# A transformer block in float32 on one core: large products split into four column tiles

## The chip, the cores and the metric

The kernel runs on one core of a Trainium2 chip. The metric is the device time of one execution in microseconds, the median over several runs. The core has a matrix engine (TensorE, "PE" in the profile, its weight loads "PEld"), a vector engine (DVE), a scalar engine (ACT), GpSimd (POOL) and a queue engine (SP) that starts most transfers.

## The reference

The kernel computes one pre-norm transformer block over 16 sequences of 256 tokens with 256 features, all in float32:

```python
def reference(x, wq, wk, wv, wo, gate_cp, up_cp, down_cp):
    x = x + attn(layernorm(x), wq, wk, wv, wo)
    return x + ffn(layernorm(x), gate_cp, up_cp, down_cp)

def attn(x, wq, wk, wv, wo):                 # 16 heads of 16
    q, k, v = x @ wq.T, x @ wk.T, x @ wv.T   # split in heads
    scores = einsum("bihd,bjhd->bhij", q, k) * 16 ** -0.5
    scores = where(j - i > 16, -inf, scores) # no key over 16 ahead
    return einsum("bhij,bjhd->bihd", softmax(scores), v) @ wo.T

def ffn(h, gate_cp, up_cp, down_cp):         # inner width 1024
    gate_w, up_w, down_w = (spline(cp) for cp in ...)  # cubic splines through control points
    return (silu(h @ gate_w.T) * (h @ up_w.T)) @ down_w.T
```

## The kernel before

One sequence is a batch b. The weights of the feed-forward part are made once at the start from the control points (`spline`) and stay in SBUF. The rest is a software pipeline: the loop over s (20 steps) does, in each step, stages of several batches that are at different points of their way. An order written out by hand says which stage stands where: within a step there are seven gaps between blocks of scores, and `project` and `fill` put the other products into them. Every engine runs its instructions in the order in which they are written (`InOrder`), so this order is what each engine does.

A full step has on PE, roughly: scores (`inner`), values (`values`, tile po), gate and up products (`gate_up`, tiles pg and pu), scores, query and key products (`project_part`, pq and pk), scores (`outer`), pg and pu, scores, po, pg and pu, scores, output projection (`project_o`, py), first half of the down product (`down`, pd), scores, second pd, transposes of the normed tokens (`turn_f`, ptf), value projection (`project_v`, pv), transposes of the maxima (`turn_max`, pm), pg and pu. For the first seven batches the normed input is transposed on PE too (`turn_a`, pta); later ones load a transposed input and are scaled afterwards. Three small sums of weights (`sum_weights`) occur once.

PE works on these in different shapes. The scores use 16 or 17 rows (the head's width, and one more for the maximum) and 64 columns, eight in the array side by side. The values use 128 rows and 32 columns, four side by side: the four heads of a group write to partitions 0, 32, 64 and 96 of the tile po:

```python
pe.matmul(
    po[32 * r : 32 * r + 32, gg, i : i + n],
    lhsT=vs[b % NQK][:, c, 4 * g + r, :],
    ...
```

All the large products use the whole array, 128 rows by 128 columns, with 256 columns streamed, and the transposes of normed tiles use `pe.transpose`, a matrix instruction in a transposing mode, against the tile `ident`. In the profile a float32 product shows as two instructions, a transpose as one.

PSUM is shared by pools: two tiles for the scores (`ps_s`), two buffers for pg, pu, pd and the splines (`ps_f`), two for everything else (`ps_m`). ACT computes the exponentials (e), the tanh of the gate (th) and several copies; DVE the row maxima (z), the gate's products (th, inter) and the residual sums.

Of the kernel before, what the change touches and what calls it, by code (L numbers as in the profile page):

```python
# [18 lines left out]
P = 128  # L19
# [74 lines left out]
def block_kernel(  # L94
# [14 lines left out]
    pe, dve, act, pool, sp = (  # L109
        InOrder(tc, e) for e in (nc.tensor, nc.vector, nc.scalar, nc.gpsimd, nc.sync)  # L110
    )
# [21 lines left out]
    xTs = {}  # L133
# [7 lines left out]
    w_in = {}  # L141
# [28 lines left out]
    ident = const.tile([P, P], F32, tag="ident", name="ident")  # L170
# [3 lines left out]
    means = const.tile([P, P], F32, tag="means", name="means")  # L174
# [37 lines left out]
    downT = const.tile([P, 8, DIM], F32, tag="downT", name="downT")  # L212


    xns, mxs, aus, aos, recs, x2s, x2Ts = ({} for _ in range(7))
# [15 lines left out]
    def normed(b, nm):  # L231
# [6 lines left out]
            )  # L238
        return xn

    def copied(engine, dst, src):
        (act.copy if engine is act else dve.tensor_copy)(dst, src)

    def transposed(src, dst, nm, engine=act):

        pt = ps_m.tile([P, 2, S], F32, tag="m", name=f"p{nm}")
        for kc in range(2):
            for c in range(2):
                pe.transpose(
                    pt[:, kc, c * P : (c + 1) * P],  # L250
                    src[:, c, kc * P : (kc + 1) * P],
                    ident,
                )
        copied(engine, dst, pt)


# [11 lines left out]
    def turn_a(b, engine=act):  # L268
        xTs[b] = sb3.tile([P, 2, S], F32, tag="xT", name=f"xT{b}")
        transposed(xns.pop(b), xTs[b], f"ta{b}", engine)  # L270

    sums = {}

    def sum_weights(nm):
        sums[nm] = ps_f.tile([P, DIM], F32, tag="f", name=f"sum{nm}")
        for kc in range(2):
            pe.matmul(
                sums[nm], lhsT=means, rhs=w_in[nm][:, kc, :], start=(kc == 0), stop=(kc == 1)
            )

    def center(nm):
        for kc in range(2):
# [16 lines left out]
    def project_part(b, i):  # L299

        if i == 0:
            qkcs[b] = sb.tile([P, 2, 2, S], F32, tag="qkc", name=f"qkc{b}")
        nm, qkc = "qk"[i], qkcs[b]
        pq = ps_m.tile([P, 2, S], F32, tag="m", name=f"p{nm}{b}")
        for oc in range(2):
            for kc in range(2):
                pe.matmul(
                    pq[:, oc, :],
                    lhsT=w_in[nm][:, kc, oc * P : (oc + 1) * P],
                    rhs=xTs[b][:, kc, :],  # L310
                    start=(kc == 0),
                    stop=(kc == 1),
                )
        if b < RAW:
            act.copy(qkc[:, i], pq)
        else:
            dve.tensor_tensor(
                qkc[:, i], pq, across[b].unsqueeze(1).to_broadcast([P, 2, S]), ALU.mult
            )

    def project_qk(b):
        project_part(b, 0)
        project_part(b, 1)
# [11 lines left out]
    def project_v(b, engine=act):  # L335
        pv = ps_m.tile([P, 2, DIM], F32, tag="m", name=f"pv{b}")
        for c in range(2):
            for kc in range(2):
                pe.matmul(
                    pv[:, c, :],  # L340
                    lhsT=xTs[b][:, kc, c * P : (c + 1) * P],
                    rhs=w_in["v"][:, kc, :],
                    start=(kc == 0),
                    stop=(kc == 1),
                )
        for c in range(2):
            to = vs[b % NQK][:, c, :, 0:HD]
            heads = pv[:, c, :].rearrange("p (h d) -> p h d", d=HD)
            if b < RAW:
                copied(engine, to, heads)  # L350
            else:
                act.activation(to, heads, AF.Copy, scale=factors[b][:, c : c + 1])
        del xTs[b]
# [177 lines left out]
    def project_o(b):  # L531
        py = ps_m.tile([P, 2, DIM], F32, tag="m", name=f"py{b}")
        ao = aos.pop(b)
        for c in range(2):
            for kc in range(2):
                pe.matmul(
                    py[:, c, :],
                    lhsT=ao[:, kc, c * P : (c + 1) * P],
                    rhs=w_in["o"][:, kc, :],
                    start=(kc == 0),  # L540
                    stop=(kc == 1),
                )
        dve.tensor_tensor(xs[b], xs[b], py, ALU.add)

# [6 lines left out]
    def turn_f(b):  # L551
        x2Ts[b] = sb.tile([P, 2, S], F32, tag="x2T", name=f"x2T{b}")
        transposed(x2s.pop(b), x2Ts[b], f"tf{b}")


    def gate_up(b, i):
        if i == 0:
            inters[b] = sb1.tile([P, 8, S], F32, tag="inter", name=f"inter{b}")
        pp = []
        for nm, w in (("g", gateT), ("u", upT)):  # L560
            t = ps_f.tile([P, 2, S], F32, tag="f", name=f"p{nm}{b}_{i}")
            for ic in range(2):
                for kc in range(2):
                    at = (2 * i + ic) * P
                    pe.matmul(
                        t[:, ic, :],
                        lhsT=w[:, kc, at : at + P],
                        rhs=x2Ts[b][:, kc, :],
                        start=(kc == 0),
                        stop=(kc == 1),  # L570
                    )
            pp.append(t)
        th = sb.tile([P, 2, S], F32, tag="th", name=f"th{b}_{i}")
        act.activation(th, pp[0], AF.Tanh, scale=0.5)
        dve.scalar_tensor_tensor(th, th, 1.0, pp[0], ALU.add, ALU.mult)
        dve.tensor_tensor(inters[b][:, 2 * i : 2 * i + 2, :], th, pp[1], ALU.mult)

    pds = {}

    def down(b, c, half=None):  # L580

        inter = inters[b]
        if half != 1:
            pds[b, c] = ps_f.tile([P, DIM], F32, tag="f", name=f"pd{b}_{c}")
        for ic in range(8) if half is None else range(4 * half, 4 * half + 4):
            pe.matmul(
                pds[b, c],
                lhsT=inter[:, ic, c * P : (c + 1) * P],
                rhs=downT[:, ic, :],
                start=(ic == 0),  # L590
                stop=(ic == 7),
            )
        if half == 0:
            return
        dve.tensor_tensor(xs[b][:, c, :], xs[b][:, c, :], pds.pop((b, c)), ALU.add)
        to = out[b].rearrange("(c p) d -> p c d", p=P)
        if b == B - 1:
            sp.dma_start(to[:, c, :], xs[b][:, c, :])
        elif c == 1:
            sp.dma_start(to, xs.pop(b))  # L600
# [48 lines left out]
    def fill(s, gap):  # L649


        if s < B - AHEAD:
            order = (
                (1, gate_up, 1), (3, gate_up, 2), (4, gate_up, 3), (5, down, 0), (6, down, 1),
            )
        else:
            order = (
                (1, gate_up, 1), (2, gate_up, 2), (3, gate_up, 3), (4, down, 0, 0),
                (5, down, 0, 1), (6, down, 1, 0), (6.5, down, 1, 1),
            )  # L660
        for at, stage, *what in order:
            if at == gap:
                do(stage, s - 4, *what)
        if gap == 7:
            do(gate_up, s - 3, 0)
# [3 lines left out]
    def part(i):  # L669
# [6 lines left out]
            (stats_a, 2), (scores_and_values, 2),  # L676
        ),
        (0, 4): ((turn_a, 1, dve), (project_v, 0, dve), (norm_a, 2), (part, 0)),
        (1, 1): ((turn_a, 2), (project_part, 1, 0), (stats_a, 3)),
        (1, 2): ((project_part, 1, 1), (spread, 1), (coefficients, 1)),  # L680
        (1, 3): ((project_qk, 2), (spread, 2), (norm_a, 3), (scores_and_values, 3)),
        (1, 4): ((project_v, 1), (stats_a, 4)),
        (1, 5): ((turn_a, 3), (part, 1), (norm_a, 4), (coefficients, 2)),
        (1, 6): ((project_qk, 3),),
        (1, 7): (
            (spread, 3), (stats_a, 5), (norm_a, 5), (project_v, 2), (part, 2),
            (scores_and_values, 4),
        ),
# [8 lines left out]
        (3, 2): ((project_qk, 6), (spread, 6)),  # L697
        (3, 3): ((project_v, 4), (project_v, 5)),
        (3, 6): ((project_v, 6), (sum_weights, "q"), (sum_weights, "k")),
        (3, 7): ((center, "q"), (center, "k")),  # L700
        (4, 1): ((sum_weights, "v"), (center, "v")),
    }

# [27 lines left out]
    for s in range(B + 4):  # L731
# [20 lines left out]
        fill(s, 4)  # L752
        inner(nb, tb, 3)
        do(project_o, ob)
        do(stats_f, ob)
        project(s, 5)
# [46 lines left out]
```

## Time and profile before

| | |
|---|---|
| time, median of 3 runs | 657.59 us (655.72 to 658.88) |
| the profiled execution, its own time | 656.36 us |
| its span, first to last instruction | 654.3 us |
| PE busy, matrix instructions | 644.9 us, 7380 |
| PEld busy | 501.3 us |
| DVE, ACT, POOL busy | 369.0, 216.3, 129.5 us |
| granted clock of TensorE | 1.000 |
| PE's program fetched (queue q8) | 58 packets, 0.95 MB |
| large products in the timeline: pg, pu, pd | 512 instructions each |
| pq, pk, pv, py | 128 instructions each |
| ptf and pta; pm | 64 and 28; 32 |
| po; scores | 1024; 4096 |

Nearly all instructions carry line 88, that of the helper `InOrder`, so groups are told apart by the names of their tiles: "pg<-x2T,gateT" writes pg from x2T and gateT. The form stands behind it: 128*32 is an instruction on 128 rows and 32 columns of the array, and 128x256 says what it streams. Matrix instructions overlap, so the lengths that the timeline gives run into each other; what a stage takes is read from its start to the start of the next one.

### The profile page before, as it was taken

How to read it: one execution, taken by the hardware profiler on the slowest of the kernel's cores; microseconds unless marked ns; L12 is line 12 of the kernel's file. 1: busy time of each engine (PE TensorE's matmuls, PEld its weight loads, DVE VectorE, ACT ScalarE, POOL GpSimd, SP SyncE). 2: the span in 40 equal slices, each digit the busy share in tenths (PEclk: the TensorE clock that was granted, in tenths of full speed). 3: DMA queues.
4: the chain of work that ended last, by engine and by line, in shares of the span. 5: the costliest groups of instructions: out<-in, count | busy, mean ns of one | idle time of the engine just before them, and what ended most of it. 6: DMA issues, size and time to landing. Idle time of an engine off the chain costs nothing.

```text
span 654.3 us, 18421 instructions
## 1 busy us (share of the span) xinstructions
PE 644.9 (99%) x7380; PEld 501.3 (77%) x7380; DVE 369.0 (56%) x1482; ACT 216.3 (33%) x383; POOL 129.5 (20%) x254
## 2 busy tenths in 40 slices
PE   8999999999999999999999999999999999999998
PEld 6666667877878777787877778787777777777886
DVE  6785566656464665646566464655656564733342
ACT  1345533233332323333232333323333333333110
POOL 6232222211111221112121121211212030212000
PEclk9999999999999999999999999999999999999999
DMA  5844132214132231413213131210010101010100
GB/s 170 174 69 63 46 64 65 46 37 87 31 75 42 45 65 36 86 33 73 44 36 75 36 71 33 56 31 18 21 34 20 33 23 31 23 36 19 50 17 16
DMA packets 40612, 33.18 MB, mean 51 GB/s; under 512 B 10576, under 2 KB 39888, under 8 KB 40528
## 3 DMA queue, kind: packets, MB, share of 16 engines
q1 hardware_dynamic: 39392, 30.97, 21.3%
q8 instruction: 58, 0.95, 0.6%
q10 hardware_dynamic: 1136, 1.05, 0.6%
q14 instruction: 26, 0.21, 0.3%
HBM read 14.42 MB, written 4.47 MB: 29 GB/s over the span
## 4 chain that ended last, share of the span: by engine, by line
PE 89%; DVE 1%; ACT 1%; issue 0%; POOL 0%; ACTq 0%
PE pg L88 18%; PE pd L88 17%; PE pu L88 17%; PE scores L88 14%; PE po L88 7%; PE py L88 5%; PE pv L88 3%; PE pq L88 3%; PE pk L88 3%; PE ptf L88 1%; PE pw L88 1%; PE pm L88 0%; ACT e L88 0%; DVE z L88 0%; DVE x L88 0%
## 5 line engine op out<-in xcount | busy, mean ns | idle before, releaser
L88 ACT ACTIVATE e<-scores 128x512 f32<-128x512 f32 (+1 forms) x192 | 117.5, 615 | 273.1 <-PE scores L88 224.5
L88 DVE CUSTOM_DVE_ANT_0 z<-scores,mask 128x144 bf16<-128x144 f32 (+1 forms) x512 | 154.7, 362 | 55.5 <-PE scores L88 32.7
L88 POOL TENSOR_SCALAR_AFFINE_SELECT e<-e 128x224 f32<-128x224 f32 (+1 forms) x192 | 93.8, 489 | 407.2 <-ACT e L88 404.4
L88 PE MATMUL pg<-x2T,gateT 128*128 128x256 f32 x512 | 125.5, 388 | 0.1
L88 PE MATMUL pu<-x2T,upT 128*128 128x256 f32 x512 | 121.0, 379 | 0.0
L88 PE MATMUL pd<-downT,inter 128*128 128x256 f32 x512 | 119.4, 383 | 0.0
L88 DVE SCALAR_TENSOR_TENSOR th<-th,pg 128x512 f32<-128x512 f32 x64 | 44.0, 687 | 117.5 <-ACT th L88 117.5
L88 PE MATMUL scores<-qk 17*64 17x144 f32 (+7 forms) x4096 | 106.2, 317 | 1.6 <-ACT e L88 1.1
L88 PEld LDWEIGHTS pg<-x2T,gateT 128*128 128x128 f32 x512 | 92.5, 190 | 19.7 <-DVE mx L88 4.7
L88 PEld LDWEIGHTS pu<-x2T,upT 128*128 128x128 f32 x512 | 97.3, 190 | 13.2
L88 PEld LDWEIGHTS pd<-downT,inter 128*128 128x128 f32 x512 | 95.2, 190 | 14.5 <-DVE mx L88 0.9
L88 PEld LDWEIGHTS scores<-qk 17*64 17x64 f32 (+1 forms) x4096 | 68.8, 131 | 37.3 <-issue 31.1
L88 ACT ACTIVATE th<-pg 128x512 f32<-128x512 f32 x64 | 38.2, 597 | 69.8 <-PE pg L88 69.2
L88 DVE TENSOR_TENSOR inter<-th,pu 128x512 f32<-128x512 f32 x64 | 44.0, 688 | 26.2 <-PE pu L88 26.2
L88 PE MATMUL po<-e,v 128*32 128x256 f32 (+1 forms) x1024 | 50.0, 336 | 0.0
L88 PEld LDWEIGHTS po<-e,v 128*32 128x32 f32 x1024 | 29.5, 109 | 23.3 <-issue 12.3
L88 DVE DVE_READ_ACCUMULATOR2_ANT mx<- 128x1 f32 x512 | 42.6, 83 | 0.1
L88 DVE TENSOR_TENSOR x<-x,pd 128x256 f32<-128x256 f32 x32 | 13.4, 420 | 41.2 <-PE pd L88 39.9
L88 PE MATMUL pq<-xT,wq 128*128 128x256 f32 x128 | 31.7, 390 | 0.7 <-ACT xT L88 0.7
L88 PE MATMUL py<-wo,ac 128*128 128x256 f32 x128 | 31.9, 392 | 0.0
L88 PE MATMUL pv<-wv,xT 128*128 128x256 f32 x128 | 30.7, 384 | 0.4 <-ACT qkc L88 0.4
L88 PE MATMUL pk<-xT,wk 128*128 128x256 f32 x128 | 30.6, 381 | 0.0
(69 smaller groups left out, 382.9 us busy)
## 6 DMA issues: line engine op xcount, KB each, us to landing
qk<-qkc SPq DMA_DIRECT2D x124, 64.0 KB
x<-x SPq DMA_DIRECT2D x16, 256.0 KB
ac<-au SPq DMA_DIRECT2D x128, 32.0 KB
rb<-rd SPq DMA_DIRECT2D x32, 128.0 KB
out<-x SPq DMA_DIRECT2D x15, 256.0 KB
xT<-xT SPq DMA_DIRECT2D x9, 256.0 KB
fa<-ra SPq DMA_DIRECT2D x9, 128.0 KB
qk<-mxT SPq DMA_DIRECT2D x64, 4.0 KB
```

What stands on the lines that cost most here:

```text
L88: return self.tc.keep_in_program_order(fn(*args, **kwargs))
```

## The change

A helper `product` writes one large product as four matrix instructions, for the columns 0 to 31, 32 to 63, 64 to 95 and 96 to 127 of its stationary operand; each writes its 32 partitions of the output. The moving operand is the same for all four. `project_part`, `project_v`, `project_o`, `gate_up`, `down` and `sum_weights` call it. The transposes of normed tiles (`transposed`, called by `turn_a` and `turn_f`) become products with `ident` as the moving operand, by the same helper. `turn_max` keeps its transposes, the splines and the few warm-up products at the start (`keep_running`) keep their forms, and the scores and values are as they were.

```diff
+    def product(out, lhsT, rhs, start, stop):
+        for at in range(0, P, 32):
+            pe.matmul(
+                out[at : at + 32], lhsT=lhsT[:, at : at + 32], rhs=rhs, start=start, stop=stop
+            )
+
+    def turned(out, src):
+        product(out, src, ident, True, True)
+
...
-                pe.transpose(
-                    pt[:, kc, c * P : (c + 1) * P],
-                    src[:, c, kc * P : (kc + 1) * P],
-                    ident,
-                )
+                turned(pt[:, kc, c * P : (c + 1) * P], src[:, c, kc * P : (kc + 1) * P])
...
-                    pe.matmul(
-                        t[:, ic, :],
-                        lhsT=w[:, kc, at : at + P],
-                        rhs=x2Ts[b][:, kc, :],
-                        start=(kc == 0),
-                        stop=(kc == 1),
+                    product(
+                        t[:, ic, :], w[:, kc, at : at + P], x2Ts[b][:, kc, :], kc == 0, kc == 1
                     )
...
-            pe.matmul(
-                pds[b, c],
-                lhsT=inter[:, ic, c * P : (c + 1) * P],
-                rhs=downT[:, ic, :],
-                start=(ic == 0),
-                stop=(ic == 7),
+            product(
+                pds[b, c], inter[:, ic, c * P : (c + 1) * P], downT[:, ic, :], ic == 0, ic == 7
             )
```

The other calls (pq, pk, pv, py and the sums) are changed in the same way.

More of the change, by code (lines that the diff above doesn't have):

```diff
@@ L276, in sum_weights @@
         for kc in range(2):
-            pe.matmul(
-                sums[nm], lhsT=means, rhs=w_in[nm][:, kc, :], start=(kc == 0), stop=(kc == 1)
-            )
+            product(sums[nm], means, w_in[nm][:, kc, :], kc == 0, kc == 1)
     def center(nm):
@@ L306, in project_part @@
             for kc in range(2):
-                pe.matmul(
-                    pq[:, oc, :],
-                    lhsT=w_in[nm][:, kc, oc * P : (oc + 1) * P],
-                    rhs=xTs[b][:, kc, :],
-                    start=(kc == 0),
-                    stop=(kc == 1),
+                product(
+                    pq[:, oc, :], w_in[nm][:, kc, oc * P : (oc + 1) * P], xTs[b][:, kc, :],
+                    kc == 0, kc == 1,
                 )
@@ L338, in project_v @@
             for kc in range(2):
[L339 to L344, printed above, removed]
+                product(
+                    pv[:, c, :], xTs[b][:, kc, c * P : (c + 1) * P], w_in["v"][:, kc, :],
+                    kc == 0, kc == 1,
                 )
@@ L535, in project_o @@
             for kc in range(2):
[L536 to L541, printed above, removed]
+                product(
+                    py[:, c, :], ao[:, kc, c * P : (c + 1) * P], w_in["o"][:, kc, :],
+                    kc == 0, kc == 1,
                 )
@@ L564, in gate_up @@
                     at = (2 * i + ic) * P
-                    pe.matmul(
-                        t[:, ic, :],
-                        lhsT=w[:, kc, at : at + P],
-                        rhs=x2Ts[b][:, kc, :],
-                        start=(kc == 0),
-                        stop=(kc == 1),
+                    product(
+                        t[:, ic, :], w[:, kc, at : at + P], x2Ts[b][:, kc, :], kc == 0, kc == 1
                     )
@@ L585, in down @@
         for ic in range(8) if half is None else range(4 * half, 4 * half + 4):
-            pe.matmul(
-                pds[b, c],
-                lhsT=inter[:, ic, c * P : (c + 1) * P],
-                rhs=downT[:, ic, :],
-                start=(ic == 0),
-                stop=(ic == 7),
+            product(
+                pds[b, c], inter[:, ic, c * P : (c + 1) * P], downT[:, ic, :], ic == 0, ic == 7
             )
```

## The prediction

> **What bounds the kernel now.** I read the page from the top: the share of each engine, then the chain that ended last, then the groups of the matrix engine, and last its timeline over one full batch.
>
> ```profile
> span 654.3 us, 18421 instructions
> PE 644.9 (99%) x7380; PEld 501.3 (77%) x7380; DVE 369.0 (56%) x1482; ACT 216.3 (33%) x383; POOL 129.5 (20%) x254
> PEclk9999999999999999999999999999999999999999
> ...
> PE 89%; DVE 1%; ACT 1%; issue 0%; POOL 0%; ACTq 0%
> ```
>
> PE is busy in 99% of the span at its full granted clock (1.000 in the view of the cores), and nearly all of the chain is PE. No other engine comes near: whatever PE's stages gain or lose goes into the end time one for one, if the other engines keep their slack. So the question is what PE does between useful columns. The timeline of PE shows it (start, length, instructions; the lengths overlap, so I read start to start):
>
> ```profile
> 304.17 1.89 PE L88 MATMUL pu<-x2T,upT 128*128 128x256 f32 x8
> 305.99 1.04 PE L88 MATMUL scores<-qk 16*64 16x208 f32 x32
> 306.96 1.56 PE L88 MATMUL po<-e,v 128*32 128x256 f32 x32
> 308.45 1.99 PE L88 MATMUL pg<-x2T,gateT 128*128 128x256 f32 x8
> 310.28 1.89 PE L88 MATMUL pu<-x2T,upT 128*128 128x256 f32 x8
> ...
> 319.52 3.72 PE L88 MATMUL pd<-downT,inter 128*128 128x256 f32 x16
> 323.08 0.60 PE L88 MATMUL ptf<-ident,xnf 128*128 128x128 f32 x4
> 323.51 1.89 PE L88 MATMUL pv<-wv,xT 128*128 128x256 f32 x8
> 325.24 0.38 PE L88 MATMUL pm<-ident,mx 128*16 128x128 f32 x2
> 325.46 1.89 PE L88 MATMUL pg<-x2T,gateT 128*128 128x256 f32 x8
> ```
>
> Three forms of the array alternate: 128*128 (the large products and transposes), 128*32 (po, the values: four side by side), 16*64 and 17*64 (scores). Each logical f32 product is two instructions (8 in a stage of four products). pv between ptf and pm takes 323.51 to 325.24, 1.73 us for 8: 216 ns each, no gap. pg after po takes 308.45 to 310.28, 1.83: about 0.10 more. pu before the scores takes 304.17 to 305.99, 1.82: about 0.09 more. These tenths are changes of form.
>
> The single starts in the trace make them exact; they repeat to within a few ns all along the span.
> - From the last start of a 128*128 stage to the scores: 309 ns, so 93 beyond its 216. All 94 such exits lie between 93 and 106.
> - From the scores' last columns to a large product: 86 (68 times). Then the product's first instruction takes 320 ns instead of 216: 104 of exposed weight load (128 columns). A transpose exposes 56 (3 times).
> - From the scores to po: 86 (31 times), and then only 24 of exposed load (32 columns per tile).
> - From po to a large product or transpose: 94 (30 times), and then 104 or 55.
> - Inside po, four tiles start 7 ns apart, and the next four follow 216 ns after the first four for 256 columns: the same pace as one full product of 256 columns.
>
> **The change part by part.** The built program keeps the order of every engine; waits and signals of PE's stages stay on the first and last instruction of each. DVE, ACT, POOL and the DMA queues issue what they did, so what follows is PE's alone. It adds 3 tiles to each of 2,048 large instructions (+6,144), turns 92 transposes into 736 (+644) and 12 sums into 48 (+36): 7,380 matrix instructions become 14,204, with as many loads.
>
> 1. Columns streamed by the large products: 216 ns for four tiles against 216 for one. Cost 0. A rule speaks against it. The Trainium skill, "TensorEngine Tiling (Array Packing)", Instruction Overhead, gives each matmul some 60 cycles[...]. At 2.4 GHz (the clock in "TensorE: Matmul & The Clock Gate", the table at its head) that is 25 ns; 6,180 added tiles would cost 155 us, an estimate, if they add up, and the time would be 815. The po row says that they don't: the tiles of a group overlap. I take the row.
>
> 2. Scores to product: exposed load 104 becomes 24, 68 times, and 56 becomes 24 for 3 transposes: -5.5 us.
>
> 3. Values to product: same form now, so 94 + 104 go, and also the 20 ns by which the fourth tile lags: -218 ns x 29, and -170 for one transpose: -6.5 us.
>
> 4. Products to scores: the last tile starts 3 x 7 = 20 ns after the first, so the change of form begins later: +20 ns x 94 = +1.9 us. I take 93 for the change itself, as out of either form.
>
> 5. The transposes. A transposing instruction of 128 columns takes 109 ns (ptf: 323.08 to 323.51 for four). A product by the identity is two instructions of that length: the warm-up products on ident run 111 apart, and 14 of them are 28 instructions. So 4 x 109 more for each of 16 ptf and 7 pta stages: 23 x 0.436 = +10.1 us. It lies on PE's own path in all but the first pta. For x2T the ACT copy (0.59 us) then starts 0.44 later; pv, 1.73 us, covers that where it stands between. Where it doesn't, PE already waits for the copy, and the 0.44 is in the sum.
>
> 6. turn_max keeps its transposes (pm). pv, pm and pg follow each other with no gap now (325.24 to 325.46 is two instructions of 109). So pm runs in the full form and its neighbours no longer do. The trace has no transposing instruction beside 128*32 work, so I bound it: 0 if a transpose needs no form of its own, and 20 + 93 + 5 on entry and 93 + 24 - 2 on exit if it does. The same page (Restrictions) says that column tiling excludes the f32 transpose. By the row alone both ends are possible; with the page it is the upper one, and I take it: 14 x 118 + 15 x 115 = +3.4 us, and 0 for the low end.
>
> 7. The few stages that start after an idle wait, and the one step from products to values: -0.4 us.
>
> Sum: -5.5 - 6.5 + 1.9 + 10.1 + 3.4 - 0.4 = +3.0 us. The profiled execution lasted 656.36 us (its span of 654.3 and 2.1 around it), 1.2 below the median of the three runs, 657.59. So 659.4 for the profiled one and 660.6 for the median: 0.46% more.
>
> What is late next if PE's products start earlier? In the batch shown, pg after po starts 0.2 us sooner, but DVE's th of the chunk before had freed its buffer at 305.68, 2.7 us ahead of 308.45; pd waits for inter, done at 312.90, 2.0 us ahead of its 314.90. The least slack is ACT's copy of x2T, done at 324.30 for pg at 325.46: 1.16 us, of which the longer transposes take 0.44, less what pv and pm grow. Nothing new should come late.
>
> **The rivals.**
>
> Transpose without a form: step 6 is 0, the sum -0.4, so 657.2. For it: no gap around pm now. Against it: the rule quoted above. Chance 0.26.
>
> Leaving the narrow form is cheap (the other side). The exit from 128*32 to the scores is never seen without a wait in this trace; both times PE stood 0.54 us for ACT's e. The 113 ns of step 4 could be less, down to none, if narrow tiles drain one by one while the scores load. Free exits give 94 x 113 = -10.6, so 650.0. It decides for faster when an exit costs under about 45 ns. Against it: po to pg, the other exit from the narrow form, costs the full 94. Chance 0.10.
>
> PE's instruction supply. PE's program is fetched in pieces of 16 KB (q8: 58 packets, 0.95 MB), one for every 256 instructions; it will need about 111. The products now draw 8 instructions each 216 ns, 37 per us, and the whole kernel 28,408 in 657 us, 43 per us on average against 22. In its favour as a danger: the densest 5 us of the trace show 47 per us and no long stretch shows more, and these fetches take 0.9 to 2.6 us in the DMA records. Against: 64 pairs of scores run in 1.07 us (318.45 to 319.52), far denser, without a gap. If each of the 53 added fetches held PE for half a microsecond, it would be +26 us; a tenth of that is +3, so about 664. Chance of 3 us or more: 0.16.
>
> That the tiles do not run side by side is excluded by po, which has the same tile positions.
>
> **How the numbers follow.** A difference of 0.5%, 3.3 us, is about what a measurement of this kernel can tell from no change: below 654.3 is faster, above 660.9 slower. The main case (0.48) centres on 660.6, with 2 us either way for the spread of the runs, for a switch out of the narrow form of 86 rather than 93 and for some fetches: a little less than half of it is slower, the rest the same. The case without a form for pm is nearly all the same. The cheap exit is faster, the supply slower. That gives 0.12 faster (with 0.02 from the edges), 0.48 the same, 0.40 slower. The range reaches from 655 (half the exits' price gone, or pm free and a run at the low edge) to 667 (the main case with 6 us of fetch stalls).
>
> **What would show each step.** pg, pu and pd at x2048 with four starts per 216 ns (step 1); pg after po beginning 0.1 us after po's last group and lasting 1.73 (step 3); pg after scores 1.75 instead of 1.84 (step 2); pu to scores 1.84 instead of 1.82 (step 4); ptf at x512, 0.87 us a stage instead of 0.43 (step 5); pm's stage with about 0.23 us more around it (step 6). Wrong would be: a stage of 8 product groups longer than 1.75 with PE waiting for "issue", which is the supply; exits to the scores under 45 ns; or DVE or ACT releasing PE where it waits for nothing now.

## The result, and the profile after

The changed kernel takes 681.99 us (median of 4 runs, 675.34 to 690.64) against 656.78 for the kernel before, a ratio of 1.0346 (95% interval 1.0263 to 1.0429): 23 to 25 us slower, where 3 were forecast. Ratios, here and below, leave out slow runs (here the profiled execution itself, 690.64, and in e1_quiet one of 683.94), so sizes below come from stretches of the profiled execution, not from its total. The profiled executions of e7_wide and e10_no_fa, below, show the same stops.

From its page: span, busy times, granted clock, the queue that fetches PE's program, and the chain.

```profile
span 688.6 us, 32067 instructions
PE 666.1 (97%) x14204; PEld 394.5 (57%) x14204; DVE 368.4 (54%) x1482; ACT 216.8 (31%) x383; POOL 130.5 (19%) x254
PEclk9999899899999999999999998999999999999999
q8 instruction: 112, 1.84, 1.2%
PE 87%; issue 2%; DVE 1%; SPq 1%; ACT 1%; DMA 0%; POOL 0%; DVEq 0%; ACTq 0%
```

PE's instructions are the 14,204 expected and the fetches 112. Two things are new against the page of before: "issue" on the chain, time in which PE waits for nothing that the profile shows, has 2% where it had 0%, and there are slices in which the clock is not full (mean 0.977 instead of 1.000).

First a stretch without them, PE's timeline late in the span:

```profile
468.17 3.66 PE L88 MATMUL pd<-downT,inter 128*32 128x256 f32 x64
471.65 1.06 PE L88 MATMUL ptf<-ident,xnf 128*32 128x128 f32 x32
472.52 1.91 PE L88 MATMUL pv<-wv,xT 128*32 128x256 f32 x32
474.36 0.39 PE L88 MATMUL pm<-ident,mx 128*16 128x128 f32 x2
474.68 1.93 PE L88 MATMUL pg<-x2T,gateT 128*32 128x256 f32 x32
476.43 1.91 PE L88 MATMUL pu<-x2T,upT 128*32 128x256 f32 x32
478.27 1.04 PE L88 MATMUL scores<-qk 16*64 16x208 f32 x32
479.24 1.56 PE L88 MATMUL po<-e,v 128*32 128x256 f32 x32
480.62 1.91 PE L88 MATMUL pg<-x2T,gateT 128*32 128x256 f32 x32
482.35 1.91 PE L88 MATMUL pu<-x2T,upT 128*32 128x256 f32 x32
```

Here every step of the forecast stands. pg after po lasts 1.73 (was 1.83), and po itself 1.38 until pg starts (was 1.49). pu before the scores lasts 1.84 (was 1.82). ptf lasts 0.87 (was 0.43). pv and pm with the changes of form around them last 2.16 (was 1.95). From one pm to the next, a late batch takes 33.33 us where the kernel before takes 33.30: 0.03 more, the forecast's own balance for a batch.

The same place of the program one batch earlier, where the transfers of the early batches still run:

```profile
418.42 3.63 PE L88 MATMUL pd<-downT,inter 128*32 128x256 f32 x64
421.98 0.97 PE L88 MATMUL scores<-qk 16*64 16x80 f32 x45
426.33 1.01 PE L88 MATMUL scores<-qk 16*64 16x144 f32 x19 [3.38 <-issue]
427.27 6.05 PE L88 MATMUL pd<-downT,inter 128*32 128x256 f32 x64
```

In the middle of a block of scores, after 45 of 64, PE stands for 3.4 us, and then the second pd needs 5.9 us until the next stage instead of 3.5. This is the sign that the prediction named for the supply of instructions: PE waiting for "issue". The windows of this stretch give the reason of the second (columns: us, busy time and instructions of each engine, granted clock, DMA share, GB/s):

```profile
418.00:422.00 4.00, 4.00 (x79) 2.20 (x72) 2.31 (x10) 0.38 (x1) 1.07 (x2) 1.00 0.13 14
422.00:426.00 4.00, 0.95 (x49) 0.68 (x45) 1.07 (x3) 0.00 (x0) 0.00 (x0) 0.92 0.05 7
426.00:432.00 6.00, 5.67 (x67) 2.96 (x71) 1.92 (x16) 1.30 (x2) 1.28 (x2) 0.50 0.01 4
432.00:436.00 4.00, 4.00 (x90) 2.45 (x82) 0.42 (x1) 0.59 (x2) 0.00 (x0) 0.98 0.20 66
```

The clock is at half after the stop, and while it is, the same columns take twice as long. In the whole execution 30.7 us lie at half clock between 30 and 640 us of the span, none in the kernel before. For the stop itself there is this line in the transfers of 416 to 426:

```profile
q8 instruction: 1, 0.02, 4.5%
```

One fetch, 16 KB of PE's program, whose packet took 4.5% of 16 engines x 10 us = 7.2 us. Over all 112 the mean is 1.2% x 16 x 688.6 / 112 = 1.2 us. In the records it runs from 417.7 to 424.9; at 426.3 PE goes on. In other batches the late fetch is short (0.9 us) but begins up to 250 instructions of PE later than its neighbours. The place of the stops fits an end of the fetched program: by the records of PE's queue, those of 1.69, 2.64, 0.56 and 3.38 us come after 8,642, 10,434, 12,226 and 17,346 instructions, and these numbers differ by whole multiples of 256, the length of one fetch. The list of SP's transfers has one entry just ahead of the long fetch that turned out to matter:

```profile
415.08 0.54 SPq L88 DMA_DIRECT2D ra<-rstda  x1
```

ra is the write of a batch's 256 scaling factors to DRAM (`send_factors`), turned by the access pattern `"(c p) -> p c"` into 256 pieces of 4 bytes.

PE's waits for "issue" (total us, times, longest) are these; the view of before has none on PE itself:

```profile
PE scores L88 <- issue: 9.8, 6, 3.4
PE pd L88 <- issue: 3.7, 3, 2.6
```

Of the 30.7 us at half clock, 23.9 follow these stops. The other 6.8, at 66.9 us, come before the first of them, and e8_mixed_spaced below has the same stretch at 66.4 us without any stop for "issue", so they are not the supply's. 13.5 us of stops and 30.7 us at half clock, of which half is lost, make 29, of which the supply has 25. With the forecast's 3, the 29 are nearly the whole distance of this execution from the one before (690.6 - 656.4 = 34).

### The profile page after: what moved, and what is told of

Read it like the earlier page. It is cut to its first block, busy times and chain, and to the rows that moved or that the text cites. A ratio compares the mean times of both kernels' runs of the same rounds, so it can differ in the third digit from the quotient of the medians.

```text
span 688.6 us, 32067 instructions
## 1 busy us (share of the span) xinstructions
PE 666.1 (97%) x14204; PEld 394.5 (57%) x14204; DVE 368.4 (54%) x1482; ACT 216.8 (31%) x383; POOL 130.5 (19%) x254
## 2 busy tenths in 40 slices
DMA packets 40666, 34.06 MB, mean 49 GB/s; under 512 B 10576, under 2 KB 39888, under 8 KB 40528
## 3 DMA queue, kind: packets, MB, share of 16 engines
q8 instruction: 112, 1.84, 1.2%
## 4 chain that ended last, share of the span: by engine, by line
PE 87%; issue 2%; DVE 1%; SPq 1%; ACT 1%; DMA 0%; POOL 0%; DVEq 0%; ACTq 0%
PE pd L88 18%; PE pg L88 16%; PE pu L88 16%; PE scores L88 14%; PE po L88 7%; PE py L88 4%; PE pv L88 3%; PE pk L88 3%; PE pq L88 3%; PE ptf L88 2%; PE pw L88 1%; PE pm L88 1%; SPq L88 1%; DMA rb<-rd 0%; ACT e L88 0%
## 5 line engine op out<-in xcount | busy, mean ns | idle before, releaser
L88 PE MATMUL pd<-downT,inter 128*32 128x256 f32 x2048 | 130.0, 402 | 3.8 <-issue 3.7
L88 PE MATMUL pg<-x2T,gateT 128*32 128x256 f32 x2048 | 123.0, 381 | 0.1
L88 PE MATMUL pu<-x2T,upT 128*32 128x256 f32 x2048 | 122.2, 379 | 0.0
L88 PEld LDWEIGHTS pd<-downT,inter 128*32 128x32 f32 x2048 | 68.5, 116 | 53.0 <-issue 16.7
L88 PEld LDWEIGHTS pu<-x2T,upT 128*32 128x32 f32 x2048 | 66.6, 110 | 43.9
L88 PEld LDWEIGHTS pg<-x2T,gateT 128*32 128x32 f32 x2048 | 62.9, 110 | 41.0 <-issue 3.4
L88 PE MATMUL pq<-xT,wq 128*32 128x256 f32 x512 | 30.9, 382 | 0.7 <-ACT xT L88 0.7
L88 PE MATMUL py<-wo,ac 128*32 128x256 f32 x512 | 30.9, 382 | 0.6 <-DVE ac L88 0.6
L88 PE MATMUL pv<-wv,xT 128*32 128x256 f32 x512 | 31.3, 380 | 0.2 <-ACT qkc L88 0.2
L88 PE MATMUL pk<-xT,wk 128*32 128x256 f32 x512 | 30.6, 380 | 0.0
```

The lines of the kernel that those rows point to most:

```text
L88: return self.tc.keep_in_program_order(fn(*args, **kwargs))
```

## The experiments

Theories: *supply* (PE's program comes late, and the clock falls after the stop), *rate* (PE can't take in so many instructions, whatever the transfers), *form* (the narrow form itself lowers the clock). For all runs I compare the time of a batch, from one pm's start to the next in the profiled execution; each batch is numbered by the pm at its end.

| kernel | median us | ratio to before, 95% | batches 4 to 10, us |
|---|---|---|---|
| before | 655.9 to 658.8, measured again beside each group of runs | | 38.48 all |
| changed | 682.0 | 1.0346 (1.0263 to 1.0429) | 39.2 to 45.1 |
| e1_quiet | 671.9 | 1.0195 (1.0149 to 1.0242) | 38.5 to 40.1 |
| e2_spaced | 669.2 | 1.0186 (1.0144 to 1.0229) | 38.5 to 40.3 |
| e3_mixed | 652.9 | 0.9933 (0.9916 to 0.9949) | 38.09 all |
| e4_transposes | 679.8 | 1.0354 (1.0306 to 1.0402) | 38.6 to 44.1 |
| e5_quieter | 663.4 | 1.0074 (1.0044 to 1.0103) | 38.51 all |
| e6_no_factors | 665.7 | 1.0102 (1.0056 to 1.0148) | 38.51 all |
| e7_wide | 674.8 | 1.0272 (1.0224 to 1.0321) | 38.3 to 44.3 |
| e8_mixed_spaced | 653.6 | 0.9933 (0.9905 to 0.9961) | 38.09 all |
| e9_no_ra | 660.2 | 1.0068 (1.0045 to 1.0090) | 38.51 all |
| e10_no_fa | 682.4 | 1.0385 (1.0354 to 1.0416) | 39.1 to 44.7 |
| e11_after_row | 662.7 | 1.0091 (1.0057 to 1.0124) | 38.52, one 38.88 |
| e12_wide_row | 651.6 | 0.9917 (0.9893 to 0.9940) | 37.91 all |

Batches 12 to 15 run while no input, factors or queries are moved any more, and are undisturbed in all of these kernels (33.33 in the changed kernel), at the full rate of instructions and the full clock. That spoke against *rate* and *form* from the start.

**Is it the supply?** e1_quiet leaves out most of the moved data:

```diff
     def spread(b):
         qkc = qkcs.pop(b)
+        if b >= RAW:
+            return
...
     def load_xT(b):
-        xTs[b] = sb3.tile([P, 2, S], F32, tag="xT", name=f"xT{b}")
-        sp.dma_start(xTs[b], xT[b].rearrange("(kc p) t -> p kc t", p=P))
+        if b == RAW:
+            held["xT"] = sb3.tile([P, 2, S], F32, tag="xT", name="xTheld")
+            sp.dma_start(held["xT"], xT[b].rearrange("(kc p) t -> p kc t", p=P))
+        xTs[b] = held["xT"]
```

> The changed kernel with most of the steady transfers left out: from the eighth batch on, queries and keys are not spread (8 x 64 KB a batch) and the transposed input is loaded once and used again, so the results of those batches are not the reference's; PE's instructions are the same, all of them. Supply theory (PE's program, fetched in pieces of 16 KB, waits behind bursts of data on the same DMA engines, PE stands still, and its clock falls after it): no stop over 0.5 us after the first steps, no half-clock stretch there, each batch within 0.1 us of the time of the kernel before, 658 to 666 us. Rate theory (the narrow form asks for more instructions than PE can take in): as slow as the changed kernel, 675 to 690. Form theory (the narrow form itself lowers the clock): half-clock stretches stay, 670 to 690.

Measured: 671.9. Stops are fewer and shorter (1.5 us at most) and no batch has a half clock, but the level is missed. Some fetches still took 3 us, one of them at 359.6 us with no data packet on any DMA engine beside it. *Supply* is half right: data had something to do with it, but bursts of data beside the fetch are not what delays it.

e2_spaced keeps all transfers and places them apart:

```diff
...
-            (spread, pb, 2),
+            (spread_first, pb, 2),
             (send_factors, pb + 1, 2),
-            (load_xT, pb + 1, 4),
+            (spread_second, pb, 5),
+            (load_xT, pb + 1, 7),
```

> The changed kernel with the same transfers placed apart: of the eight transfers that spread queries and keys, four stay where they are and four go three gaps later, and the load of the transposed input goes from gap 4 to gap 7. Supply theory: the longest burst is halved, so most stops of over 1 us go and with them the half-clock stretches: 660 to 670. Rate or form theory: no change, 675 to 690.

Measured: 669.2, as expected in number. Fetches of 2.2 to 3.9 us stay. By what follows, the reading behind the number was wrong: bursts were not the cause, they made it worse.

**Which transfer?** From batch 9 on, e5_quieter leaves out ra and fa besides what e1_quiet does; e6_no_factors leaves out only ra and fa; e9_no_ra only ra; e10_no_fa only fa, the broadcast that brings ra's row to all partitions (128 KB).

```diff
     def send_factors(b):                      # e5, e6 and, with the old row kept for fa, e9
         _, factors[b] = moments.pop((b, "a"))
+        if b > RAW:
+            return
...
     def spread_factors(b):                    # e5, e6, e10
-        to = sb3.tile([P, S], F32, tag="fa", name=f"fa{b}")
-        sp.dma_start(to, across[b].unsqueeze(0).to_broadcast([P, S]))
-        across[b] = to
+        if b == RAW:
+            to = sb3.tile([P, S], F32, tag="fa", name=f"fa{b}")
+            sp.dma_start(to, across[b].unsqueeze(0).to_broadcast([P, S]))
+            held["fa"] = to
+        across[b] = held["fa"]
```

> As e1_quiet, and from the ninth batch on the scaling factors are not sent through DRAM and spread (a write of 256 pieces of 4 bytes, ra, and a broadcast of 128 KB, fa, a batch), so those batches are not the reference's. In e1_quiet one fetch of PE's program in each early batch still took some 3 us with no data packet beside it, often soon after ra, and PE stood 0.3 to 1.7 us behind it. Theory that the small writes of ra hold the fetch up: those long fetches go, each batch within 0.1 us of the kernel before, 658 to 664 us. Theory that what remains (rb, the loads of x, the stores) or the place in the program does it: long fetches stay in the steps up to the twelfth, 666 to 675.

> The changed kernel with only ra and fa left out from the ninth batch on (those batches are not the reference's); the spread of queries and keys and the loads of the transposed input stay. If the small writes are the main hold-up: 658 to 667. If the burst of queries, keys and input is: stops of 1 to 4 us stay in most of the early batches, 670 to 685.

e5 gave 663.4, e6 665.7; in both every batch from the fourth to the eleventh takes 38.51. In e6 all queries, keys and inputs are moved as in the changed kernel: their bursts alone do no harm. The one ra that both still write, the eighth batch's, is followed by the one stop for "issue" that they have left, 2.7 us in e5 and 3.6 in e6.

> The changed kernel with only the write ra left out from the ninth batch on (256 pieces of 4 bytes to DRAM, one a batch); the broadcast fa is read from the eighth batch's row instead, so those batches are not the reference's. Queries, keys and input are moved as before. Theory that ra's small writes hold up the fetches of PE's program that follow: no stop from step 5 on, 38.51 us a batch, 658 to 666. Theory that the broadcast fa does it: stops stay, 672 to 690.

> The changed kernel with ra written as before, and only the broadcast fa (128 KB) left out from the ninth batch on (those batches use the eighth's factors and are not the reference's). By the theory of ra's writes the stops stay as they are: 672 to 690, fetches of 3 to 8 us soon after ra. By the theory of fa they go: 658 to 666.

e9 gave 660.2, e10 682.4. The two differ in a write of 1 KB a batch (and in which of them has the broadcast). PE's timeline of e9 at the place of the stop:

```profile
398.41 1.14 PE L88 MATMUL scores<-qk 16*64 16x80 f32 x64
399.48 3.66 PE L88 MATMUL pd<-downT,inter 128*32 128x256 f32 x64
402.96 1.06 PE L88 MATMUL ptf<-ident,xnf 128*32 128x128 f32 x32
```

and of e10, and its write ra from SP's list:

```profile
416.80 0.97 PE L88 MATMUL scores<-qk 16*64 16x80 f32 x45
420.37 1.00 PE L88 MATMUL scores<-qk 16*64 16x144 f32 x19 [2.60 <-issue]
421.30 3.21 PE L88 MATMUL pd<-downT,inter 128*32 128x256 f32 x28
```

```profile
409.34 0.54 SPq L88 DMA_DIRECT2D ra<-rstda  x1
```

The scores break off after the same 45 instructions in e10 as in the changed kernel: the program has reached the end of what was fetched. In e9 they run through. With ra gone the changed kernel costs about what the forecast said: 4.3 us more than the kernel before, measured beside it (655.9), where 3.0 was forecast. Two stops of 1.4 and 0.5 us are left in its first 101 us. That 660.2 meets the forecast median of 660.6 more closely is in part luck, as the kernel before was 1.7 us faster there than the 657.6 that the forecast started from.

The records also show for how long ra holds the fetches up. In the changed kernel, the kernel before, e3, e4 and e7, 45 writes of ra in all, no fetch ends between 3.4 and 8.9 us after an ra is issued (in e10 one does, in nine). At the eight places where e9 leaves ra out, a fetch ends in that time at every one.

**Does the amount of fetching matter?** e3_mixed takes the kernel before and makes only the stages after the values narrow; e7_wide also the other products between two blocks of scores.

```diff
...
                     product(
                         t[:, ic, :], w[:, kc, at : at + P], x2Ts[b][:, kc, :], kc == 0, kc == 1,
+                        i == 1 or (i == 3 and b < B - AHEAD - 4),   # e3; in e7: i > 0
                     )
...
```

In both, `product` has one more argument, narrow or not, and the transposes are those of before.

> The kernel before, with only those products in the narrow form that follow the values: gate and up of chunk 1 and of chunk 3 (in the last steps the first half of the first down product in place of chunk 3), transposes as before. By the sum of the prediction each of some 28 places gains 218 ns on entry and loses 20 on exit: -5.5 us, so about 651 where the kernel before has 656.8. Supply theory: only some 2,700 instructions are added to 14,800, PE's program asks for 68 fetches instead of 58, stops are rare: 650 to 653. Form theory: the clock falls here too, over 657.

> As e3_mixed, and also narrow: every other product that stands between two blocks of scores (query and key products from the eighth batch on, chunk 2 of gate and up, output projection, first down product); the second down product, the transposes, the value projection, the maxima and chunk 0 stay full. In an undisturbed batch three more stages save 80 on entry and lose 20 on exit: 0.18 us less than e3_mixed (37.91 where the kernel before has 38.48 and e3_mixed 38.09). Without stops that is about 649. PE's instructions are some 23,000, between e3_mixed (17,500) and the changed kernel (28,400). Supply theory: stops come back in the early batches, about a third to a half of the changed kernel's 25 us: 655 to 663. If supply only fails above this rate: 648 to 651.

e3 gave 652.9: faster than before by 0.7%, and 0.39 us a batch, as two times 218 - 20 ns should. PE's timeline there shows both forms side by side:

```profile
305.07 1.56 PE L88 MATMUL po<-e,v 128*32 128x256 f32 x32
306.45 1.91 PE L88 MATMUL pg<-x2T,gateT 128*32 128x256 f32 x32
308.18 1.91 PE L88 MATMUL pu<-x2T,upT 128*32 128x256 f32 x32
310.02 1.04 PE L88 MATMUL scores<-qk 16*64 16x208 f32 x32
310.99 1.99 PE L88 MATMUL py<-wo,ac 128*128 128x256 f32 x8
```

e7 gave 674.8 with undisturbed late batches of 32.73 (33.30 before) and stops as long as in the changed kernel, 4.2 us in its timeline:

```profile
255.50 1.10 PE L88 MATMUL scores<-qk 16*64 16x80 f32 x54
260.85 0.46 PE L88 MATMUL scores<-qk 17*64 17x144 f32 x10 [4.24 <-issue]
```

That missed its expectation: with 89 fetches instead of 112 the loss is as large, 23 us against the same forms without ra (e12 below). With 69 fetches (e3) there is none to be seen. So the harm sets in between these two and is not in proportion. e3's fetches were late at times too, one took 4.5 us: PE then still had instructions in hand. How much it has in hand can be estimated. The large stops come some 250 instructions after the count at which a fetch usually begins (the median in the changed kernel), so a fetch has about the time of one block of 256 to arrive. That is the span divided by the fetches: 11.3 us in the kernel before, 9.4 in e3, 7.3 in the forms of e7 (by e12, below) and 5.9 in those of the changed kernel (by e9). The longest fetch took 7.2 us in the changed kernel and 8.4 in e7: a block that lasts 11 or 9 us outlives that, one of 7 or 6 does not. This is an estimate from means; no run varies the rate alone.

e8_mixed_spaced, e3_mixed with e2_spaced's order, changes nothing (653.6, the same ratio as e3):

> e3_mixed with the transfers placed apart as in e2_spaced. In e3_mixed a batch already runs at its undisturbed time, so there is little left for it: 651 to 653, no more than 1 us under e3_mixed. Were stops still hidden in e3_mixed's unprofiled runs, up to 2 us.

**The transposes.** e4_transposes puts `pe.transpose` back in `transposed`:

> The changed kernel with the transposes of normed tiles put back to transposing instructions in the full form. By the sum of the prediction: 0.44 us less for each of 23 stages, but each stage now enters and leaves the full form: 20 + 93 + 56 on entry and 93 + 24 on exit where narrow work stands on both sides, 0.29 us. So about 0.15 us less a batch in an undisturbed stretch (33.18 where the changed kernel has 33.33 in batches without a value projection before the maxima; a little different by neighbours). The stops stay as they are: 672 to 690 by the supply theory; by the theory that the added transposing products cost the time, 657 to 665.

679.8, and late batches of 33.19 where the changed kernel has 33.33: 0.14 less, with 0.15 forecast. The transposing products are a loss by themselves, but of about 3 us in all (an estimate, 0.14 for each of the 23 stages), and no cause of the 25.

**Without the small write.** e11_after_row and e12_wide_row send the factors another way, in the changed kernel and in e7_wide:

```diff
     def send_factors(b):
         _, factors[b] = moments.pop((b, "a"))
-        across[b] = dr.tile([S], F32, tag="ra", name=f"ra{b}")
-        sp.dma_start(across[b].rearrange("(c p) -> p c", p=P), factors[b])
+        dve.tensor_copy(mxs[b - 5][:, :, H], factors[b])
...                             # spread_factors, which read ra, is gone
     def turn_max(b):                # rows = H + 1 where the batch b + 5 has factors
...
+        if rows > H:
+            across[later] = sb3.tile([P, S], F32, tag="fa", name=f"fa{later}")
+            sp.dma_start(across[later], mxT[H : H + 1, :].unsqueeze(1).to_broadcast([1, P, S]))
```

> The changed kernel, whole, without small writes: the factors of a batch go as a seventeenth column into the tile of the maxima that turn_max transposes anyway, and the row that comes out is spread to all partitions by one transfer; ra is gone. If ra is the whole of the loss: 659 to 663, as e9_no_ra (660.2), 38.51 to 38.6 us a batch. If the new spread from one partition holds the fetches or the maxima's transfers up in its turn: stops of over 0.5 us in the early batches, over 665.

> e7_wide (narrow only where it saves: products between two blocks of scores, and after the values) with the same way for the factors. Undisturbed batches of 37.91 to 38.0 instead of e7_wide's 38 to 46: 647 to 651, under e3_mixed (652.9) and the kernel before. If supply still fails at this rate without ra: over 653.

e11: 662.7, 0.9% or 4.9 us above before, so the whole kernel, with the factors of every batch, comes within 2 us of the forecast's 3.0 once the write is gone. One stop of 0.8 us is left in its start. e12: 651.6, 0.8% below, with no stop on PE for "issue" left; from its page:

```profile
span 648.4 us, 26174 instructions
PE 638.4 (98%) x11268; PEld 424.9 (66%) x11268; DVE 369.1 (57%) x1491; ACT 216.1 (33%) x383; POOL 129.6 (20%) x254
```

e12 and e3 both beat the two kernels of this study; their intervals overlap, so which is better stays open.

## Why the prediction was wrong

The sum of seven steps was right, to the ns where the trace can show it: no cost for four tiles (1), 80 ns saved on each entry from the scores (2), no change of form after the values (3), 20 ns at each exit (4), 0.44 us a transposing stage (5), 0.21 to 0.23 around pm, whose transposes do need the full form (6). e9_no_ra, where nearly only this sum is left, has a profiled time of 660.47, within 1.1 us of the 659.4 forecast for a profiled execution.

The step that failed is the one that put the fetches at next to nothing: "the DMA queues issue what they did, so what follows is PE's alone". The queue that brings PE's program issues twice what it did, and in place of nothing the profiled execution shows 13.5 us of stops and some 12 us lost to the half clock behind them. The prediction had this as the rival "PE's instruction supply", and weighed it wrongly in three ways. It had 0.16 of the chance and a price of "about 664", though the changed kernel must fetch at twice the rate and the trace of before held no long stretch at that rate; the honest price reached to the +26 written beside it. Its argument against, 64 pairs of scores in 1.07 us, shows that PE can issue quickly what it has in hand; it says nothing on whether the next 16 KB arrive in time. And the mechanism was not the number of fetches: it is single fetches, one in a batch, that come 3 to 7 us late after ra. That the measured loss is so near the +26 is luck: that figure assumed half a microsecond at each of 53 fetches, and the trace has nine stops and a slower clock after five of them. The half clock was nowhere in the working; in the profiled execution (mean clock 0.977) it is nearly half of the loss, and by the same working a fifth to a half of it in the others (0.982 to 0.995).

What could have been read before: in the DMA records of before, fetches 11, 18 and 36 took 2.3 to 2.6 us, of 58 with a median near 1.0, and others began up to 150 instructions late. Each of the three begins 8 to 10 us after an ra. For the last of them, SP's list of before and the transfers of 396 to 400 say:

```profile
388.51 0.54 SPq L88 DMA_DIRECT2D ra<-rstda  x1
q8 instruction: 1, 0.02, 3.5%
```

3.5% of 16 engines x 4 us are 2.2 us; the fetch ends 10.9 us after the ra. At one fetch in 11 us that was slack. The prediction used the 0.9 to 2.6 as a harmless range and didn't ask what precedes the long ones.

Not tried, and open: the path by which ra holds up a fetch. Its packets take 9 ns each in the records and are over before the late fetch begins. The Trainium skill, "DMA: Bandwidth & Descriptors", Specifications, says that below 512 B a transfer becomes a read-modify-write, which would fit; these runs show only that the harm goes with the write. Being small is not enough by itself: e11 still moves 8,128 packets under 512 B, of 10,576 in the changed kernel, and has no stop for "issue" after 93 us. No run writes ra in larger pieces, or moves it to another place among the transfers. Open too is why the bursts of queries and keys make it worse when ra is there (682 with them, 671.9 without), when without ra they do nothing (660.2). In e1 and e2, where they are gone or moved, fetches do end 4 to 9 us after an ra, so with the bursts in place the time in which none arrives is longer.

## What to carry to other kernels

Before multiplying an engine's instructions, look at the queue that fetches its program: how many fetches, how long they take and which of them are late now, and what late ones would cost at the new rate. Then look at what stands in the DMA list ahead of the late ones. A PE that is 99% busy hides nothing, and a stop of a few us can also cost the clock for some us after it. Narrow forms pay where they join a stage of the same form; make those narrow first, and count the instructions that each further one adds.

## What the hardware showed beyond expectation

- A write of 256 pieces of 4 bytes to DRAM, 1 KB a batch, cost 22 us in 682 by delaying program fetches (e9 against e10), though its own packets take 9 ns each.
- A stop of 0.9 us (at 342 us of the changed kernel's span) was followed by 3.4 us at half clock, one of 3.4 us by 6.8 us; stops of 1.9 and 2.3 us (at 100 and 213 us of e10_no_fa's) by none. In the changed kernel all six stretches at half clock last 3.4 us or twice that, and begin a whole multiple of 3.41 us after the first: it starts at 66.9 us, the others 64.9, 150.2, 194.6, 276.5 and 358.4 us later, which is 19, 44, 57, 81 and 105 times 3.41. So where a stop falls on this grid seems to decide with its length; no run shifts a stop to show it.
- A transposing instruction with 16 columns between narrow products pays 93 to 94 ns of change of form on both sides, so it counts as the full form.
- Four tiles of 128 by 32 keep the pace of one full product over runs of 64 instructions: 216 ns for each four.
